# Ordering the scatters of pairs, and normalizing the first two batch elements beside the last expert slots

## The chip, the cores and the metric

One Trainium2 chip; the kernel runs on one of its cores. The metric is the device time of one launch in microseconds (us), as the median over several runs. A core has five engines that each follow their own instruction stream: TensorE (PE in the profile), VectorE (DVE), ScalarE (ACT), GpSimd (POOL) and SyncE (SP). Transfers run on 16 DMA engines and are started by instructions on SP or POOL.

## The reference

Causal attention with 16 heads over four batch elements of 1024 rows of 256 numbers, a layer norm, a mixture of experts (8 experts, each row uses two), and a second layer norm. Cut to what matters here:

```python
# x: (4, 1024, 256)
x = layernorm(x + attention(x))
scores = (x @ router_w.T + router_b) / temp
gates  = sinkhorn(scores)                      # 3 rounds
vals, idx = top_k(gates, 2)
g   = relu(einsum('btd,edf->btef', x, wg))     # wg, wp: (8, 256, 512)
p   = einsum('btd,edf->btef', x, wp)
all = einsum('btef,efd->bted', g * p, wo)      # wo: (8, 512, 256)
x = layernorm(x + sum over the two chosen experts of gate * all)
```

## The kernel before

**Attention.** The four batch elements are worked through in turn. After the attention of an element come its projection, residual and first layer norm (L547 to 557); the normalized rows are stored to two DRAM tables, `x_rows` (what the experts gather) and `results` (what they add to). Then `route` (L688 to 839) works out the gates, the two experts of each row, and the place of each of the 2048 (row, expert) pairs in a DRAM table `pairs`, which holds a region for each expert. `scatter` (L842 to 856) writes these pairs: 16 indirect DMAs per element, issued by POOL. A small hand-written planner (`Lane`, L1061) decides where in the instruction stream each piece is put: a generator yields the cost of what it has just issued (`SCAT`, `SCAT3`, or 1.0 for the last element) and the places in the attention, or in the slots, call `give(budget)`. The Tile scheduler then reorders within the dependencies.

**Slots.** An expert's rows are handled in slots. The lists are
- `first[0..7]`: 512 rows of each expert, from elements 0 to 2 only, so that they can run while the last element is still being routed;
- `second[0..7]`: the next 512 rows of each expert, with rows of all elements, in the fixed order 7, 6, ... 0. The first of them is the same expert as `first[7]` and takes over its split weights (`like`, L1116). All eight pair lists come with one DMA of 64 KB (`ents1`, L977);
- `further`: slots of 256 rows, whose expert and list are read from a table in SBUF into SP registers. Three of them (`SURE`) are always run, any more inside `tc.If(filled > SURE)` (L1238), which this input doesn't enter.

`slot` (L1005) does gate and linear projection (`gp`, `lp`), relu times linear, and the output projection `eo`, each in three fp32r matmuls of high and low halves (L195 to 197). ACT writes the high half, DVE the low half (L188, L189). Each block of 128 output rows is added into `results` by an accumulating indirect DMA that POOL issues (L1039); the adds of a slot wait for those of the slot before (`added`). `begin` (L1204) runs in pieces between the parts of the slot ahead: it reads the pair list of the slot after next on SP, gathers its rows on POOL (L957), transposes and splits the next slot's rows, splits its weights, and loads the weights of the slot after (three DMAs of 512 KB on SP, L983). There is one raw buffer per kind of weight and two of each half, six buffers of `eo`, two of gathered rows.

**Where the last element's scatters go.** In slots `first[5]` and `first[6]`, eight `give(1.0)` each, and what is left behind `first[6]` (`places.until`, L1232). `second[0]`'s list can be read only when the last of them has landed.

**The end.** After the last slot's adds: eight loads of 512 rows (`z`, L1255, SP), statistics on DVE (L1269, L1270), `rstd` and `off` on POOL (L1272 to 1276), normalization on ACT for the first five (L1279) and on DVE for the last three (`DZ` = 3, L1287), and the stores (L1258, SP).

Of the kernel before, what the change touches and what calls it, by code (L numbers as in the profile page):

```python
# [21 lines left out]
XG = 2  # L22
SCAT, SCAT3 = 3.5, 2.5
DZ = 3
HB = 6
# [16 lines left out]
def kernel(  # L42
# [39 lines left out]
    SR = 256  # L82
    REGION = BT + SR
    NOVER = (2 * BT - 4 * ER + 2 * (SR - 1)) // SR
    NLIST = (E - 1) * REGION + 2 * ER + NOVER * SR
# [100 lines left out]
    def split(hi, lo, src, sub=None):  # L186

        nc.scalar.copy(hi, src)  # L188
        (sub or nc.vector).tensor_tensor(lo, src, hi.bitcast(F32), ALU.subtract)  # L189

# [354 lines left out]
    def layernorm(x, n):  # L545
        mv = small.tile([P, BPQ, 2], F32, tag="mv", name=f"mv_{n}", bufs=2)
        for i in range(BPQ):  # L547
            st = small.tile([P, 6], F32, tag="bnst", name=f"bnst_{n}_{i}")
            nc.vector.bn_stats(st, x[:, i, :])
            nc.vector.bn_aggr(mv[:, i, :], st)  # L550
        rstd = small.tile([P, BPQ], F32, tag="rstd", name=f"rstd_{n}", bufs=2)
        spread[0] = nc.gpsimd.tensor_scalar_add(rstd, mv[:, :, 1], EPS_LN)
        nc.gpsimd.tensor_tensor(rstd, rstd, neg_half, ALU.pow)
        for i in range(BPQ):
            nc.vector.tensor_scalar(
                x[:, i, :], x[:, i, :], mv[:, i, 0:1], rstd[:, i : i + 1], ALU.subtract, ALU.mult
            )
# [127 lines left out]
    def route(b):  # L685
# [140 lines left out]
        yield 0.0  # L826
        nc.vector.tensor_tensor(base, base, ps[:, NE : NE + E], ALU.add)
        if b == B - 2:
            nc.vector.tensor_tensor(base, base, floor, ALU.max)
# [12 lines left out]
    def scatter(b, ent, ati):  # L842

        for n in range(NB):
            for k in range(2):
                while not hole[0]:
                    yield WAIT
                ins = nc.gpsimd.indirect_dma_start(  # L848
                    out=pairs[:, :],
                    out_offset=bass.IndirectOffsetOnAxis(ap=ati[:, k, n : n + 1], axis=0),  # L850
                    in_=ent[:, n, k, :], in_offset=None,
                )
                in_turn(ins)
                after(ins, latest[0])
                apart("pairs", "last" if b == B - 1 else "write", ins, ("last", "write", "early"))
                yield SCAT if b < B - 2 else SCAT3 if b < B - 1 else 1.0


    def tab(name, shape):
        return small.tile([1, *shape], F32, tag=name, name=name, bufs=1)  # L860

    shift = tab("shift", [E])
    for e in range(E):
        nc.gpsimd.memset(shift[:, e : e + 1], float(e * REGION + 2 * ER - SR + 1))
    tables = {}

    def lay_out():
# [35 lines left out]
        tables["filled"] = small.tile([1, 1], I32, name="filled", bufs=1)  # L903
        nc.vector.tensor_copy(tables["filled"], upto[:, E - 1 :])
        yield 0.0


    def value(r, s, top):
        return nc.values_load(
            tables["slots"][0:1, r, s : s + 1], engines=[mybir.EngineType.SP], min_val=0, max_val=top,  # L910
            skip_runtime_bounds_check_because="worked out on the chip from counts that add up to 2 * B * T",
        )
# [10 lines left out]
    class Slot:  # L923


        def __init__(self, which, s):
            self.which, self.s, self.name = which, s, f"{which}_{s}"
            self.rows = SR if which == 2 else ER
            self.blocks = self.rows // P
            self.raw, self.hl = [None] * 3, [None] * 3  # L930
            self.like = None

    lists = {}

    def pairs_of(k):
        if k.which == 2:
            row = value(1, k.s, NLIST - SR)
            k.ent = const.tile([P, k.blocks, 4], I32, name=f"ent_{k.name}")
            nc.sync.dma_start(
                out=k.ent, in_=pairs[bass.ds(row, SR)].rearrange("(p j) w -> p j w", j=k.blocks)  # L940
            )
            return
        if k.which not in lists:
            ent = lists[k.which] = const.tile([P, E, k.blocks, 4], I32, name=f"ents{k.which}")
            regions = pairs[: E * REGION].rearrange("(e r) w -> e r w", r=REGION)
            ins = nc.sync.dma_start(
                out=ent.rearrange("p e j w -> p e (j w)"),
                in_=regions[:, k.which * ER : (k.which + 1) * ER].rearrange("e (p j) w -> p e (j w)", p=P),
            )
            if not k.which:  # L950
                apart("pairs", "early", ins, ("last",))
        k.ent = lists[k.which][:, k.s]

    def gather(k):
        k.xg = early.tile([P, ER // P, C], F32, tag="xg", name=f"xg{k.name}", bufs=XG)
        for j in range(k.blocks):
            ins = nc.gpsimd.indirect_dma_start(  # L957
                out=k.xg[:, j], out_offset=None, in_=x1_rows[: BT if k.which else BT - T],
                in_offset=bass.IndirectOffsetOnAxis(ap=k.ent[:, j, 0:1], axis=0),
            )  # L960
            if not k.which:
                in_turn(ins)
# [8 lines left out]
    def weights(k, i):  # L971

        if k.like is not None:
            return
        if k.which == 2:
            if i == 0:
                k.e = value(0, k.s, E - 1)  # L977
            rows_e = bass.ds(k.e, 1)
        else:
            rows_e = slice(k.s, k.s + 1)  # L980
# [4 lines left out]
    def halves(k, i):  # L985
        if k.like is not None:
            k.hl[i] = k.like.hl[i]
            return
        w = k.raw[i]
# [14 lines left out]

    def slot(k, between):  # L1005

        R = k.rows
        hs = []
        for f in range(NFC):
# [13 lines left out]
            )  # L1023
            split(hh, hlo, r)
            hs.append((hh, hlo))
            next(between, None)
            if k in first[E - 3 : E - 1]:
                places.give(1.0)
        mine = []
        h_, l_ = k.hl[2]  # L1030
        for j in range(k.blocks):
# [17 lines left out]
            next(between, None)  # L1049
            if k in first[E - 3 : E - 1]:  # L1050
                places.give(1.0)
# [62 lines left out]
    first = [Slot(0, e) for e in range(E)]  # L1114
    second = [Slot(1, e) for e in reversed(range(E))]
    second[0].like = first[-1]  # L1116
    further = [Slot(2, n) for n in range(NOVER)]
# [79 lines left out]
    for gen in (finish(B - 1, (0,), alone=True), route(B - 1), lay_out()):  # L1197
        drain(gen)
    filled = nc.values_load(
        tables["filled"][0:1, 0:1], min_val=0, max_val=NOVER,  # L1200
        skip_runtime_bounds_check_because="worked out on the chip from counts that add up to 2 * B * T",
# [24 lines left out]

    def run(keys, given=()):
        drain(begin(keys, 0, given))
        for n, key in enumerate(keys):
            slot(key, begin(keys, n + 1, given))  # L1230
            if key is first[E - 2]:
                places.until(f"S{B - 1}")  # L1232

    run(first + second + further[:SURE], (0,))

    experts.close()
    pctx.close()
    with tc.If(filled > SURE):  # L1238
        added.clear()
        with early_pool() as early, ffn_pool() as ffn:  # L1240
            run(further[SURE:])


    zp = ctx.enter_context(tc.tile_pool(name="zp", bufs=1))
    y_rows = out.rearrange("b t c -> (b t) c")
    zs = {}

    def rows_of(of, i, cut=slice(0, BPQ)):

        return of[i * QC : (i + 1) * QC].rearrange("(p n) c -> p n c", p=P)[:, cut]  # L1250

    def load_z(i):
        z = zp.tile([P, CC, FF], F32, tag="z", name=f"z{i}", bufs=BT // QC)
        z = zs[i] = z.rearrange("p k f -> p (k f)").rearrange("p (n c) -> p n c", c=C)
        nc.sync.dma_start(out=z, in_=rows_of(results, i))  # L1255

    def store_z(i, z, cut=slice(0, BPQ)):
        nc.sync.dma_start(out=rows_of(y_rows, i, cut), in_=z[:, cut])  # L1258

    n_z = BT // QC  # L1260
    rest = []
    for i in range(n_z):
        load_z(i)
    for i in range(n_z):
        z = zs.pop(i)
        mv = small.tile([P, BPQ, 2], F32, tag="mv", name=f"mv_f{i}", bufs=2)
        for j in range(BPQ):
            st = small.tile([P, 6], F32, tag="bnst", name=f"bnst_f{i}_{j}")
            nc.vector.bn_stats(st, z[:, j, :])  # L1269
            nc.vector.bn_aggr(mv[:, j, :], st)  # L1270
        rstd = small.tile([P, BPQ], F32, tag="rstdz", name=f"rstd_f{i}", bufs=4)
        nc.gpsimd.tensor_scalar_add(rstd, mv[:, :, 1], EPS_LN / 4)  # L1272
        nc.gpsimd.tensor_tensor(rstd, rstd, neg_half, ALU.pow)
        off = small.tile([P, BPQ], F32, tag="offz", name=f"off_f{i}", bufs=4)
        nc.gpsimd.tensor_tensor(off, mv[:, :, 0], rstd, ALU.mult)
        nc.gpsimd.tensor_scalar(off, off, -1.0, None, ALU.mult)
        if i < n_z - DZ:
            for j in range(BPQ):
                nc.scalar.activation(  # L1279
                    z[:, j, :], z[:, j, :], AF.Identity, bias=off[:, j : j + 1], scale=rstd[:, j : j + 1]  # L1280
                )
            store_z(i, z)
        else:
            rest.append((i, z, rstd, off))
    for i, z, rstd, off in rest:
# [83 lines left out]
```

## Time and profile before

| | us |
|---|---|
| runs: lowest, median, highest of 3 | 1086.51, 1090.79, 1091.84 |
| the profiled execution | 1095.9 |
| its span | 1094.2 |
| attention of the four elements, about | 0 to 760 |
| first TensorE work of the second stage (`xgT` at) | 870.84 |
| adds of three alternate second slots begin | 909.83, 945.59, 981.36 |
| last add issued | 1060.81 |
| first load of z issued | 1068.04 |
| last normalization on DVE ends | 1090.73 |

Windows of the span, in us of busy time of each engine, with TensorE's granted clock as a share of its full one and the mean busy share of the DMA engines:

| stretch | PE | DVE | ACT | POOL | clock | DMA |
|---|---|---|---|---|---|---|
| 818 to 854 (36) | 35.55 | 22.00 | 19.39 | 27.17 | 1.00 | 0.53 |
| 854 to 876 (22) | 3.35 | 2.71 | 2.77 | 13.99 | 0.59 | 0.39 |
| 900 to 1020 (120) | 119.32 | 65.91 | 68.35 | 63.08 | 1.00 | 0.58 |
| 1020 to 1067 (47) | 36.54 | 20.29 | 21.70 | 21.76 | 0.92 | 0.48 |
| 1067 to 1094 (27) | 0.00 | 17.04 | 10.04 | 13.74 | 0.50 | 0.80 |

How to read such lines: a group line gives the kernel line, engine, operation, the tile written and the tile read, how often it ran, busy time and mean, and then how long the engine stood idle just before, and what ended that idle time. "SPq" is a DMA's issue on SP. In the chain of waits each piece is followed back to what released it, so the pieces add up to the span. Idle time of an engine that isn't on that chain costs nothing.

### The profile page before, as it was taken

The numbers are of one execution on the slowest core, as the hardware profiler recorded it, in microseconds if no ns is written. First come the engines' busy times: TensorE is split into PE (matmuls) and PEld (weight loads), VectorE is DVE, ScalarE is ACT, GpSimd is POOL, SyncE is SP. The second block draws the span as 40 slices with busy tenths as digits, with TensorE's granted clock in tenths as the row PEclk, the third lists the DMA queues.
The fourth block names the chain that finished last, engine by engine and source line by source line (L and its number), as shares of the span: only waits on it lengthen the run. The fifth ranks groups of instructions, "written<-read, shape, count | busy, mean of one in ns | idle before, by whom it ended". The sixth has DMA issues, their size and how long they took to land.

```text
span 1094.2 us, 18114 instructions
## 1 busy us (share of the span) xinstructions
PE 975.8 (89%) x6436; PEld 608.2 (56%) x6436; DVE 734.9 (67%) x1622; ACT 625.4 (57%) x1314; POOL 479.1 (44%) x543
## 2 busy tenths in 40 slices
PE   6689999999999999989999996899999399999970
PEld 4555433455544455543444443488888288888860
DVE  4767787888888778787757882286686145555536
ACT  3445666765665755666656663656565145555533
POOL 6177511022352632552223215427557655554535
PEclk9889999999989999999999998999999699999985
DMA  6574420231240330333143220357555345656537
GB/s 245 165 213 121 117 86 18 76 117 33 95 121 17 107 114 5 127 80 98 47 102 98 46 70 2 99 174 186 141 125 123 69 109 113 172 113 164 123 36 307
DMA packets 71363, 119.67 MB, mean 109 GB/s; under 512 B 16416, under 2 KB 43040, under 8 KB 70880
## 3 DMA queue, kind: packets, MB, share of 16 engines
q1 hardware_dynamic: 48544, 81.76, 24.3%
q0 software_dynamic: 20672, 36.41, 15.5%
q8 instruction: 53, 0.87, 0.3%
q10 hardware_dynamic: 2048, 0.27, 0.2%
q14 instruction: 46, 0.38, 0.1%
HBM read 82.52 MB, written 35.60 MB: 108 GB/s over the span
## 4 chain that ended last, share of the span: by engine, by line
PE 74%; DMA 7%; DVE 6%; ACT 5%; SPq 4%; issue 2%; POOL 2%; another core or an unknown queue 1%; ACTq 0%; POOLq 0%; DVEq 0%
PE y L436 12%; PE s L351 11%; PE sT L456 10%; SPq L336 3%; PE gp L197 3%; PE gp L196 3%; PE gp L195 3%; PE eo L197 3%; PE eo L196 3%; PE eo L195 3%; PE po L625 3%; PE lp L197 2%; PE lp L196 2%; ACT pT L467 2%; PE lp L195 2%
## 5 line engine op out<-in xcount | busy, mean ns | idle before, releaser
L467 ACT ACTIVATE pT<-sT 128x512 f32<-128x512 f32 (+1 forms) x608 | 327.1, 575 | 180.8 <-PE sT L456 129.2
L372 DVE TENSOR_REDUCE mx<-s 128x1 f32<-128x384 f32 (+3 forms) x352 | 216.6, 633 | 36.2 <-PE s L368 35.1
L351 PE MATMUL s<-ks,qs 96*128 96x512 bf16 (+3 forms) x768 | 212.4, 333 | 19.4 <-DMA ks<-parts 10.8
L456 PE MATMUL sT<-qs,ks 98*128 98x512 bf16 (+3 forms) x768 | 215.5, 330 | 9.0 <-ACT pT L467 6.9
L381 DVE TENSOR_REDUCE mx<-s 128x1 f32<-128x512 f32 x256 | 171.4, 682 | 47.6 <-PE s L351 47.1
L474 POOL TENSOR_SCALAR_AFFINE_SELECT pT<-pT 128x512 f32<-128x512 f32 x112 | 70.7, 638 | 254.9 <-ACT pT L467 250.4
L436 PE MATMUL y<-pT,va 128*32 128x512 f32 (+3 forms) x1536 | 169.2, 503 | 4.4 <-ACT pT L467 3.1
L1039 POOL DMA_INDIRECT results<-eo,ents x64 | 107.2, 1674 | 82.6 <-ACT eo L1038 65.4
L351 PEld LDWEIGHTS <-qs 96*128 96x128 bf16 x768 | 70.8, 99 | 120.3 <-issue 89.7
L456 PEld LDWEIGHTS <-ks 98*128 98x128 bf16 x768 | 69.8, 99 | 89.6 <-issue 57.4
L848 POOL DMA_INDIRECT pairs<-ent,so_i x64 | 67.8, 1060 | 75.9 <-ACT pT L467 57.5
L368 PE MATMUL s<-mask,ident_b 128*128 128x128 bf16 (+2 forms) x352 | 87.1, 248 | 0.0
L1020 DVE TENSOR_TENSOR relu<-relu,lp 128x512 f32<-128x512 f32 x64 | 43.7, 683 | 60.1 <-ACT relu L1019 30.6
L195 PE MATMUL eo<-wh,hh 128*128 128x256 f32 x280 | 80.5, 289 | 0.9 <-ACT eo L1038 0.6
L957 POOL DMA_INDIRECT xg<-x_rows,ents x64 | 65.1, 1017 | 33.6 <-issue 16.1
L196 PE MATMUL eo<-wl,hh 128*128 128x256 f32 x280 | 79.0, 284 | 0.0
L189 DVE TENSOR_TENSOR wl<-w,wh 128x512 fp32r<-128x512 f32 x108 | 69.3, 684 | 14.3 <-ACT wh L188 13.8
L197 PE MATMUL eo<-wh,hl 128*128 128x256 f32 x280 | 77.7, 284 | 0.0
L1019 ACT ACTIVATE relu<-gp 128x512 f32<-128x512 f32 (+1 forms) x76 | 42.7, 563 | 59.6 <-PE gp L197 49.9
L436 PEld LDWEIGHTS y<-pT,va 128*32 128x32 f32 x1536 | 31.8, 108 | 64.6 <-issue 46.5
L195 PE MATMUL gp<-xh,wh 128*128 128x512 f32 (+1 forms) x176 | 65.0, 376 | 2.1 <-ACT xh L188 1.2
L196 PE MATMUL gp<-xl,wh 128*128 128x512 f32 (+1 forms) x176 | 65.6, 374 | 0.0
(213 smaller groups left out, 1849.0 us busy)
## 6 DMA issues: line engine op xcount, KB each, us to landing
ks<-parts SPq DMA_DIRECT2D x90, 128.0 KB
w<-in_wg_dram SPq DMA_DIRECT2D x18, 512.0 KB
w<-in_wp_dram SPq DMA_DIRECT2D x18, 512.0 KB
w<-in_wo_dram SPq DMA_DIRECT2D x18, 512.0 KB
qs<-parts SPq DMA_DIRECT2D x66, 128.0 KB
parts<-lv POOLq DMA_DIRECT2D x12, 384.0 KB
parts<-lv POOLq DMA_DIRECT2D x24, 192.0 KB
xh<-in_x_t_dram SPq DMA_DIRECT2D x8, 512.0 KB
```

The costliest lines, as they stand in the source:

```text
L195: nc.tensor.matmul(ps, lhsT=sh, rhs=mh, start=(i == 0), stop=False)
L196: nc.tensor.matmul(ps, lhsT=sh, rhs=ml, start=False, stop=False)
L197: nc.tensor.matmul(ps, lhsT=sl, rhs=mh, start=False, stop=(i == n - 1))
L351: nc.tensor.matmul(ps, lhsT=q(h, half)[:NROW, t * P : (t + 1) * P], rhs=k(h, kc)[:NROW, :w], start=first, stop=last,)
L368: nc.tensor.matmul(each[:, :, w - P :], lhsT=ident_b, rhs=mask.unsqueeze(1).to_broadcast([P, m, P]), start=False, stop=True,)
L372: nc.vector.tensor_reduce(mx_of[:, half, h0 : h0 + m, t], each, AX.X, ALU.max)
L381: nc.vector.tensor_reduce(mx_of[:, kc, h, t : t + 1], ps, AX.X, ALU.max)
L436: nc.tensor.matmul(acc[g, qc][SLOT * h : SLOT * (h + 1), lo:], lhsT=va[b % 2][:, kb, at : at + SLOT], rhs=pT[:, h, lo:], start=(kb == 0), ...
L456: nc.tensor.matmul(st[:, h % m * w : (h % m + 1) * w], lhsT=k(h, kb // BPQ)[: NROW + 2, kb % BPQ * P : (kb % BPQ + 1) * P], rhs=q(h, qc)[: ...
L467: latest[0] = nc.scalar.activation(pT[:, h + 1 - m : h + 1, lo:], st[:, : m * w].rearrange("p (h t) -> p h t", t=w), AF.Exp, scale=scale,)
L474: diagonal[0] = nc.gpsimd.affine_select(out=block, in_=block, pattern=[[0, HG], [1, P]], compare_op=ALU.is_ge, fill=0.0, base=0, channel_m ...
L1039: ins = nc.gpsimd.indirect_dma_start(out=results[:, :], out_offset=bass.IndirectOffsetOnAxis(ap=k.ent[:, j, 1:2], axis=0), in_=eo, in_offs ...
```

## The change

1. *Scatters.* Each scatter of pairs is given a dependency on the last but one before it of the same element. `SCAT3` goes from 2.5 to 2.0. The last element's scatters cost 0.5 and not 1.0 per place, and places are given in `first[6]` only.
2. *Order of the second stage.* `order_of_second`, a few operations on one row, runs once, when element 1 has been routed. It picks the expert with the fewest rows of elements 0 and 1 and makes the eight second slots a rotation of the experts that ends with that one. Expert and list are now read into SP registers for each second slot, with one list DMA of 8 KB each; the weights of the first of them are loaded and split anew.
3. *Early end of elements 0 and 1.* In the last second slot, POOL loads the four z tiles of elements 0 and 1, after the adds of the slot before. Their statistics, `rstd` and normalization (all of it on DVE but `rstd`) and their stores on SP are put behind the last split of the further slots 0, 1 and 2. The end then has four tiles and not eight, with `DZ` = 2. If the `If` is entered, those four are loaded and normalized again after it; an expert with over 1024 rows in elements 0 and 1 (`again`) makes the program enter it.
4. In the first layer norm, the instruction that later gathers are scheduled after is the pow and not the add.

```diff
-SCAT, SCAT3 = 3.5, 2.5
-DZ = 3
+SCAT, SCAT3 = 3.5, 2.0
+DZ = 2
...
-        spread[0] = nc.gpsimd.tensor_scalar_add(rstd, mv[:, :, 1], EPS_LN)
-        nc.gpsimd.tensor_tensor(rstd, rstd, neg_half, ALU.pow)
+        nc.gpsimd.tensor_scalar_add(rstd, mv[:, :, 1], EPS_LN)
+        spread[0] = nc.gpsimd.tensor_tensor(rstd, rstd, neg_half, ALU.pow)
...
+        if b == EARLY - 1:
+            order_of_second()
...
+        sent = []
         for n in range(NB):
             for k in range(2):
...
                 after(ins, latest[0])
+                if len(sent) > 1:
+                    after(ins, sent[-2])
+                sent.append(ins)
...
-                yield SCAT if b < B - 2 else SCAT3 if b < B - 1 else 1.0
+                yield SCAT if b < B - 2 else SCAT3 if b < B - 1 else 0.5
...
+    def order_of_second():
+        few = tab("few", [E])
+        nc.vector.tensor_tensor(few, floor[:1], base[:1], ALU.subtract)
+        most, again = tab("most", [1]), tab("again", [1])
+        nc.vector.tensor_reduce(most, few, AX.X, ALU.min)
+        nc.vector.tensor_scalar(again, most, -float(ER), float(NOVER), ALU.is_lt, ALU.mult)
+        tables["again"] = again
+        nc.vector.tensor_reduce(most, few, AX.X, ALU.max)
+        nc.vector.tensor_scalar(few, few, most, None, ALU.is_equal)
...
+        nc.vector.tensor_scalar(seq[:, 1], seq[:, 0], float(REGION), float(ER), ALU.mult, ALU.add)
+        nc.vector.tensor_copy(seqi[:, 1], seq[:, 1])
...
     def pairs_of(k):
-        if k.which == 2:
-            row = value(1, k.s, NLIST - SR)
+        if k.which:
+            row = value(k.table, 1, k.s, NLIST - k.rows)
             k.ent = const.tile([P, k.blocks, 4], I32, name=f"ent_{k.name}")
             nc.sync.dma_start(
-                out=k.ent, in_=pairs[bass.ds(row, SR)].rearrange("(p j) w -> p j w", j=k.blocks)
+                out=k.ent, in_=pairs[bass.ds(row, k.rows)].rearrange("(p j) w -> p j w", j=k.blocks)
             )
             return
...
-            if k in first[E - 3 : E - 1]:
+            if k is first[E - 2]:
                 places.give(1.0)
+        if ahead is not None:
+            ahead()
         mine = []
...
-    second = [Slot(1, e) for e in reversed(range(E))]
-    second[0].like = first[-1]
+    second = [Slot(1, n) for n in range(E)]
...
+    def load_early():
+        for i in range(n_early):
+            z = work.tile([P, T], F32, tag="yT0", name=f"ze{i}", bufs=2) if i < 2 else work.tile(
+                [P, BPQ, C], F32, tag="x1", name=f"ze{i}", bufs=X1_BUFS
+            )
+            z = early_z[i] = z.rearrange("p (n c) -> p n c", c=C) if i < 2 else z
+            with tc.issue_after(further[0].gathered.ins):
+                ins = nc.gpsimd.dma_start(out=z, in_=rows_of(results, i))
+            for o in added:
+                after(ins, o)
+
+    def center_early(i):
+        mv = small.tile([P, BPQ, 2], F32, tag="mve", name=f"mv_e{i}", bufs=n_early)
+        for j in range(BPQ):
+            st = small.tile([P, 6], F32, tag="bnst", name=f"bnst_e{i}_{j}")
+            nc.vector.bn_stats(st, early_z[i][:, j, :])
+            nc.vector.bn_aggr(mv[:, j, :], st)
+        rstd = small.tile([P, BPQ], F32, tag="rstdz", name=f"rstd_e{i}", bufs=4)
+        nc.gpsimd.tensor_scalar_add(rstd, mv[:, :, 1], EPS_LN / 4)
+        nc.gpsimd.tensor_tensor(rstd, rstd, neg_half, ALU.pow)
+        early_z[i] = early_z[i], mv, rstd
+
+    def end_early(i):
+        z, mv, rstd = early_z[i]
+        for j in range(BPQ):
+            nc.vector.tensor_scalar(
+                z[:, j, :], z[:, j, :], mv[:, j, 0:1], rstd[:, j : j + 1], ALU.subtract, ALU.mult
+            )
+        store_z(i, z)
...
+    keys = first + second + further[:SURE]
+    n = keys.index(second[-1])
+    half = n_early // 2
+    run(keys, (0,), {n: load_early}, {
+        n + 1: [(center_early, i) for i in range(half)],
+        n + 2: [(end_early, i) for i in range(half)] + [(center_early, i) for i in range(half, n_early)],
+        n + 3: [(end_early, i) for i in range(half, n_early)],
+    })
```

## The prediction

> **What bounds the kernel now.** I read the page first: engine shares, then the row of granted clock.
>
> ```profile
> PE 975.8 (89%) x6436; PEld 608.2 (56%) x6436; DVE 734.9 (67%) x1622; ACT 625.4 (57%) x1314; POOL 479.1 (44%) x543
> PE   6689999999999999989999996899999399999970
> PEclk9889999999989999999999998999999699999985
> ```
>
> TensorE is busy 89% of the span, so time is found only where its row dips: slice 32 (848 to 875 us) and the last two. Windows of those places have the columns: stretch, its length, busy time of PE, weight loads, DVE, ACT and POOL, clock, DMA share, GB/s.
>
> ```profile
> 860.00:880.00 20.00, 6.94 (x27) 4.93 (x28) 1.29 (x2) 1.55 (x3) 11.99 (x13) 0.54 0.35 78
> 1035.00:1040.00 5.00, 3.37 (x22) 2.96 (x21) 3.36 (x7) 2.23 (x7) 3.39 (x2) 0.87 0.85 167
> 1055.00:1060.00 5.00, 3.70 (x25) 2.93 (x24) 0.85 (x2) 1.61 (x4) 2.03 (x2) 1.00 0.26 31
> 1060.00:1065.00 5.00, 0.00 (x0) 0.00 (x0) 0.00 (x0) 0.13 (x1) 2.05 (x2) 0.76 0.52 65
> ```
>
> There are two holes. The chain of waits over them (start, length, what):
>
> ```profile
> 862.36 2.16 DMA pairs<-ent,so_i
> 864.53 2.60 DMA ents<-pairs
> ...
> 871.82 2.54 DMA xg<-x_rows,ents
> ...
> 1054.44 3.69 DMA results<-eo,ent
> ...
> 1058.95 8.45 DMA results<-eo,ent
> ...
> 1068.90 6.47 DMA z<-results
> ...
> 1089.35 0.41 DVE z L1287
> ```
>
> The *transition* (854 to 876): the second stage cannot gather before the last element's 16 scatters of pairs have landed and the pair list is read back; TensorE stands 16.4 us and then works for some 10 us at half clock. The *tail* (1060 to 1094): the last slot's adds land at 1067.4, then 8 tiles z are loaded, normalized and stored, 26.8 us without a matmul. Everything between runs at one slot per 17.9 us with TensorE full (adds of alternate slots begin at 909.83, 945.59, 981.36).
>
> **The change part by part.** The profiled execution took 1095.9 us (span 1094.2), the median of the runs is 1090.79: a factor of 0.9953. I sum against 1095.9.
>
> *1. At most two scatters in flight, and SCAT3.* A pair scatter issues in 0.97 us with 0.30 between two and lands 2.16 after its start. Two spacings are 2.54 us, more than 2.16, so a wait for the last but one would already be over: 0. The built program's order shows no new wait on the scatters anyway, and the third element's burst of back-to-back scatters (655 to 670) is still there, six and more in a row. Cost 0.
>
> *2. The last element's scatters in one slot.* Before, POOL runs its scatters between adds from 818.6 to 863.3 without rest (scatter 0.97, add 1.58, gaps 0.30), four of them ahead of the sixth slot's first add. In the built order they start after that add (its eo is ready at 824.33) and go two by two between the adds. Filled in with the rows: add 826; four scatters to 831; two adds 835; two scatters 838; one add, two scatters 842; then eo6_0 at 845.06, and three more rounds of add plus two scatters at 4.4 us, to 863–866. POOL loses its early scatters but has the idle gap before 845 to make them up: +0.5. Behind them SP reads one 8 KB list per slot in place of one 64 KB list: between the 2.16 of a scatter and the 2.60 of the 64 KB row: −0.3. But the first three slots of `second` also queue 1 MB of weights just behind these lists, beside the gathers (landing 2.54 when nothing else ran), and ACT has the splits of that weight ahead of those of xg. At 512 KB per 3.3 us (first z of the tail: issued 1068.04, first used 1071.33) they land by 869.5 and 872, and ACT needs xg at 875: hidden, with 2 us of slack; if that goes, each microsecond is on the path, at half clock. I take **+1**, range −1 to +5.
>
> *3. order_of_second.* Thirteen operations on one row of eight numbers, 0.2 us each by routing's 128x8 rows (L756 0.214, L760 0.199), 2.7 us of VectorE once, beside attention where TensorE is 9 tenths busy and VectorE 7 to 8: 0, at most +3.
>
> *4. Second's first slot no longer borrows weights.* 1.5 MB more to load and 6 splits (ACT 0.57, DVE 0.68 each, 7.5 us together), before 875, where ACT works 1.55 and DVE 1.29 of 20 us: 0. The loads run while the seventh slot waits.
>
> *5. Rows and lists per slot.* SP now issues, per slot, list, wg, wp, wo strictly in that order. Before, every other slot's wg and wp were fetched ahead of the wo before it (wg 912.21, wp 914.01, wo 917.02). That wg moves to 918, lands by about 925, and its splits begin at 929.48: hidden, slack 4.5 us. Two register loads per slot lie in the 0.9 us that a further slot already shows between its list (1004.39) and wg (1005.29). 0, range 0 to +14 (rival C).
>
> *6. Early layer norm.* POOL now issues four loads of 512 KB (elements 0 and 1) after the adds of the last but one second slot have landed, and the last slot's adds and the gather of the third further slot stand behind them. POOL's timeline, before:
>
> ```profile
> 1027.90 1.54 POOL L1039 DMA_INDIRECT results<-eo,ents  x1 [3.67 <-DMA results<-eo,ents]
> 1036.61 2.08 POOL L1039 DMA_INDIRECT results<-eo,ents  x1 [0.31 <-ACT relu L1019]
> 1043.56 1.78 POOL L1039 DMA_INDIRECT results<-eo,ent  x1 [4.87 <-ACT hh L188]
> 1058.95 1.55 POOL L1039 DMA_INDIRECT results<-eo,ent  x1 [2.97 <-DMA results<-eo,ent]
> 1060.81 1.55 POOL L1039 DMA_INDIRECT results<-eo,ent  x1 [0.30 <-issue]
> ```
>
> Four issues at 0.84 (row of x_rows' store) put the end of issuing at 1031.3. The tail moved 2 MB in the 7 us after 1068.04; beside weights (DMA 0.62 to 0.99 busy here) I take landing at 1036.5. Here a rule bears: the Trainium skill, "DMA: Bandwidth & Descriptors", Rules for kernel authors, asks an accumulating DMA to wait for an earlier access only of the *same bytes*. The last slot's expert has no rows of elements 0 and 1, so by the rule its adds could start at 1031.3; but the built order shows the first add waiting on the four loads' semaphores. By the rule the delay of that add is 3.4 us, by the program's wait 8.6 us; I count the second. Then, with adds of 1.54 to 2.08: four adds to 1044.7, landed 1046.8; first further slot 1047.3 and 1049.2, landed 1053; second 1053.7 and 1056, landed 1060; third 1060.9 and 1063.5, landed 1070. Two of the idle gaps in the block above (4.87, 2.97) take up most of the 8.6. That is +2.7. On top come POOL's four add+pow pairs (0.23 + 1.05, gaps: 7 us over 20 us where POOL has 12 us of adds) and VectorE's 12 us (per z 1.77 for statistics, 1.38 to normalize; 4 z) in 25 us that hold 12 us of work: part of it falls ahead of relu and splits that TensorE awaits. A second rule speaks against it: "SBUF — State Buffer", Who interferes with whom, says a VectorE tensor_scalar in its two-port mode and a GpSimd operation lock each other out for the whole instruction. 16 normalizations at 0.35 would hold POOL 5.5 us if all met an add; the rows say an add takes 1.54 alone and up to 2.08 beside VectorE, so +0.5 on the two or three that matter. I take **+4** for the last add's landing in all, range +2 to +8.
>
> *7. The tail with four z.* Stores of the early z (2 MB) go beside the third further slot. Four statistics end 1.57 × 4 + about 1 after the first use, at 1078.6 had nothing moved (before: the eighth at 1086.8); POOL's four steps for the last z take 2.0 (0.23 + 1.05 + 0.22 + 0.23 and gaps), the normalization 1.4, and the end comes 3.5 after that as before: 1085.6 in place of 1094.2, **−8.5**, range −10 to −6. ACT has two z left at 2.06 each, the first two, so it is done before.
>
> Sum: +1 + 0 + 4 − 8.5 = −3.5, so 1092.4 profiled, and 1092.4 × 0.9953 = **1087.3**.
>
> **Rivals.** Case A is the sum, 1082 to 1092 from its terms' ranges.
>
> *B: an old stall goes.* The chain has 1% of "another core or an unknown queue": two stalls without a named releaser, the longer one shown here (VectorE in the third element's burst of scatters), the other ACT's 5.23 us at 705.09, during gathers.
>
> ```profile
> 669.62 0.26 DVE L604 RECIPROCAL rec<-yt_ps 128x16 f32<-128x16 f32 x1 [8.70 <-remote]
> ```
>
> Instruction packets move on two queues just there. If these are instruction fetches held up behind POOL's small descriptors, thirteen new VectorE instructions shift the place where the next block is needed. The Trainium skill, "Runtime: NRT & Kernel Launch", Instruction fetch mechanics, calls a block's cost mostly hidden; the row says 8.7. Both gone: −3.5 − 13.9, so 1073.6; the longer alone: about 1078.7. Against it: the burst itself stays, so the shift may as well leave the stall or lengthen it.
>
> *C: slower, by SP's queue in the second stage.* If the weights' slip behind wo exceeds the slack of 4.5 us (list waits, loads beside gathers of 300 GB/s), every slot is paced by its load. At 2 us for each of 7 slots, +14: 1092.4 + 14 = 1106.4, × 0.9953 = 1101. It decides from some 1.3 us per slot on, where it eats the tail's gain and 0.5% more. For it: the order has no slack between lists and weights. Against: one slot in two already runs with wg behind wo (931.4, then 932.64) and TensorE stays full.
>
> *D: the early norm is all there is.* The scatters' new places neither help nor hurt and the adds hide entirely in the gaps (+1 rather than +4): −7.5, 1083.
>
> **How the numbers follow.** What a measurement of this kernel tells from no change is about 0.5%, 5.5 us. Chances: A 0.47, B 0.15, C 0.26, D 0.12. The prediction is A's 1087. Faster by over 0.5% (under 1085.3): B 0.15, most of D 0.09, a quarter of A 0.12, so 0.36; slower: C less a little 0.24 and A's end 0.02, so 0.26; within: 0.38. The range goes down to 1075 (half of B) and up to 1100 (half of C).
>
> **What would show it.** Step 2: last scatter's start within 862 to 866, TensorE's hole 15 to 20 us. Step 5: alternate adds still 35.75 us apart. Step 6: POOL's first add of the last second slot 8 to 9 us behind the landing of the slot before, last add landed 2 to 8 us later relative to that. Step 7: 18 us from there to the end in place of 26.8. A shifted stall in the third or fourth element's attention, or a longer slot period, would make the prediction wrong.

## The result and the profile after

The changed kernel takes 1104.49 us (median of 6 runs, 1102.91 to 1105.82) and the kernel before 1089.85 (1086.51 to 1091.84): a ratio of 1.014 with a 95% interval of 1.0121 to 1.0158. It is **slower by 1.4%**. In a later set of runs, beside a median of before of 1077.86, the same pair gave 1.0103 (1.0055 to 1.0151). The profiled execution took 1105.16 us, span 1103.5, 9.3 more than that of before. The medians are 14.6 us apart; the profiled execution of before lay 6 us above its median, so the traces divide 9.3 us and not all of the 14.6.

The page after, first the lines that answer to those of before:

```profile
PE 980.0 (89%) x6436; PEld 613.6 (56%) x6436; DVE 744.0 (67%) x1654; ACT 622.7 (56%) x1308; POOL 478.5 (43%) x539
PE   6689999999999999999999986999999299999870
PEclk9899999999999999999999997899999599999985
```

TensorE's work has hardly changed (980.0 us for 975.8, same count). The dip in slice 32 has gone from 3 to 2, and the end, `970` in the last three slices before, is `870`: neither has closed. Windows (stretch, length, PE, weight loads, DVE, ACT, POOL, clock, DMA share, GB/s) of the same places:

```profile
860.00:880.00 20.00, 3.41 (x10) 2.10 (x11) 3.52 (x6) 3.36 (x6) 12.49 (x12) 0.50 0.58 174
1040.00:1060.00 20.00, 16.20 (x119) 15.62 (x119) 9.58 (x34) 7.41 (x19) 10.18 (x9) 0.91 0.53 132
1060.00:1080.00 20.00, 7.68 (x41) 6.98 (x39) 11.64 (x38) 3.12 (x8) 11.49 (x10) 0.78 0.55 122
```

TensorE finished at 1059 before; now it still has 7.68 us of work after 1060, with holes in it. Lined up on marks that both traces have, the 9.3 us divide like this. A second pair of traces, both from one later set of runs (e5 and e6 below: both kernels unchanged, spans 1078.7 and 1089.6), gives the same division:

| stretch | first pair | second pair |
|---|---|---|
| up to the last eo of `first[6]` on ACT | +0.6 | +0.5 |
| from there to the first eo of `first[7]` (the transition) | +3.4 (24.9 to 28.3) | +3.05 (25.35 to 28.4) |
| from there to the last add of the last but one second slot | −0.45 | +0.6 |
| from there to the last add of all | **+10.7** (38.7 to 49.4) | **+11.0** (36.9 to 47.8) |
| last add's start to the first load of z | +2.35 (7.2 to 9.6) | +2.7 |
| first load of z to the end | −7.3 (26.2 to 18.9) | −6.9 |

So the end did become shorter as meant, and the last four slots with the step from the last add to the first load of z gave nearly twice that back. POOL's timeline there, after:

```profile
1025.68 3.29 POOL L1069 DMA_INDIRECT results<-eo,ent  x1 [1.25 <-ACT eo L1068]
1034.60 2.25 POOL L1301 DMA_DIRECT2D ze<-results  x4 [5.64 <-DMA results<-eo,ent]
1037.15 1.09 POOL L989 DMA_INDIRECT xg<-x_rows,ent  x1 [0.30 <-PE gp L199]
...
1047.21 1.63 POOL L1069 DMA_INDIRECT results<-eo,ent  x1 [7.22 <-ACT xh L190]
...
1055.02 1.05 POOL L1314 TENSOR_TENSOR rstd_e<-rstd_e,neg_half 128x4 f32<-128x4 f32 x1
...
1060.85 1.77 POOL L1069 DMA_INDIRECT results<-eo,ent  x1 [0.20 <-issue]
1066.59 1.56 POOL L1069 DMA_INDIRECT results<-eo,ent  x1 [3.97 <-ACT hh L190]
```

The four early loads are out by 1036.85, but the add behind them starts only at 1047.21: it waits for 2 MB to land. (xh is named because ScalarE's update was the last one before the start. In the trace this add waits on the four semaphores of the early loads; in e4 below, where these waits are taken out, it follows the loads at once.) Meanwhile rstd of the early tiles (POOL) stands behind those adds, and VectorE stands at the normalization that needs rstd, with relu and splits of the last slot after it in its stream. VectorE's timeline and what TensorE waited for (engine, line, waited for: us, times, longest):

```profile
1056.10 1.38 DVE L1320 TENSOR_SCALAR ze<-ze,mv_e,rstd_e 128x256 f32<-128x256 f32 x4 [2.56 <-POOL rstd_e L1314]
1060.69 1.51 DVE L1320 TENSOR_SCALAR ze<-ze,mv_e,rstd_e 128x256 f32<-128x256 f32 x4 [3.20 <-POOL rstd_e L1314]
```

```profile
PE gp L197 <- DVE relu L1048: 5.1, 2, 4.7
PE xgT_ps L1030 <- DMA xg<-x_rows,ent: 3.3, 1, 3.3
```

TensorE waits twice that it did not before (its longest wait in these slots was 1.2 us): 3.3 us for the gather of the third further slot, which was issued behind the early loads, and 4.7 us for VectorE. After each its granted clock falls to 0.50 for some microseconds, here after the second:

```profile
1066.00:1067.00 1.00, 1.00 (x6) 1.00 (x6) 1.00 (x4) 0.51 (x2) 0.41 (x1) 0.50 0.06 16
```

### The profile page after: what moved, and what is told of

The parts are those of the page before. It is cut to its first block, busy times and chain, and to the rows that moved or that the text cites. A ratio compares the mean times of both kernels' runs of the same rounds, so it can differ in the third digit from the quotient of the medians.

```text
span 1103.5 us, 18205 instructions
## 1 busy us (share of the span) xinstructions
PE 980.0 (89%) x6436; PEld 613.6 (56%) x6436; DVE 744.0 (67%) x1654; ACT 622.7 (56%) x1308; POOL 478.5 (43%) x539
## 5 line engine op out<-in xcount | busy, mean ns | idle before, releaser
L374 DVE TENSOR_REDUCE mx<-s 128x1 f32<-128x384 f32 (+3 forms) x352 | 216.7, 633 | 36.1 <-PE s L370 35.0
L458 PE MATMUL sT<-qs,ks 98*128 98x512 bf16 (+3 forms) x768 | 216.5, 332 | 15.0 <-ACT pT L469 13.4
L383 DVE TENSOR_REDUCE mx<-s 128x1 f32<-128x512 f32 x256 | 171.3, 681 | 43.5 <-PE s L353 42.3
L191 DVE TENSOR_TENSOR wl<-w,wh 128x512 fp32r<-128x512 f32 x114 | 73.6, 684 | 37.5 <-ACT wh L190 35.0
L854 POOL DMA_INDIRECT pairs<-ent,so_i x64 | 64.7, 1011 | 72.8 <-ACT pT L469 49.2
L1069 POOL DMA_INDIRECT results<-eo,ent x38 | 64.5, 1698 | 46.6 <-ACT eo L1068 19.8
L190 ACT CAST wh<-w 128x512 fp32r<-128x512 f32 x114 | 64.0, 618 | 23.1 <-DMA w<-in_wg_dram 16.5
L1069 POOL DMA_INDIRECT results<-eo,ents x32 | 53.6, 1674 | 42.2 <-ACT eo L1068 30.2
```

The lines of the kernel that those rows point to most:

```text
L191: return (sub or nc.vector).tensor_tensor(lo, src, hi.bitcast(F32), ALU.subtract)
L374: nc.vector.tensor_reduce(mx_of[:, half, h0 : h0 + m, t], each, AX.X, ALU.max)
L383: nc.vector.tensor_reduce(mx_of[:, kc, h, t : t + 1], ps, AX.X, ALU.max)
L458: nc.tensor.matmul(st[:, h % m * w : (h % m + 1) * w], lhsT=k(h, kb // BPQ)[: NROW + 2, kb % BPQ * P : (kb % BPQ + 1) * P], rhs=q(h, qc)[: ...
L1069: ins = nc.gpsimd.indirect_dma_start(out=results[:, :], out_offset=bass.IndirectOffsetOnAxis(ap=k.ent[:, j, 1:2], axis=0), in_=eo, in_offs ...
```

## The experiments

The kernels came in four sets (e1 to e4, e5 to e8, e9 to e11, e12 and e13), each on one chip beside the kernel before, so ratios are compared and not microseconds: the median of before was 1079.37, 1077.86, 1088.75 and 1081.21. The stretches in microseconds are each from a single trace; two traces of the kernel before differ by 1.8 us in the last stretch of adds (38.7 and 36.9) and by 1.1 us from the last add to the first load of z (7.2 and 6.2).

### Which part costs it

**e1**, without the early norm (all eight z at the end, three on VectorE):

```diff
-    n_early = EARLY * T // QC
+    n_early = 0
-DZ = 2
+DZ = 3
```

> The changed kernel without its early layer norm: no z tile is loaded in the last second slot, the end has eight tiles with three on VectorE as before; scatters and order of the second stage as changed. Theory 1 (the early norm's own waits in the last slots cost more than the shorter tail brings): 1093 to 1098 us, and the adds of the last second slot follow the slot before without the 12 us hole. Theory 2 (the scatters' new places and the half clock after them cost it): stays at 1101 or above. Theory 3 (the new order's lists and weights on SP pace the second stage): also 1101 or above.

**e2**, the scatters as before, early norm and order kept:

```diff
-SCAT, SCAT3 = 3.5, 2.0
+SCAT, SCAT3 = 3.5, 2.5
-                if len(sent) > 1:
-                    after(ins, sent[-2])
-                sent.append(ins)
-                yield SCAT if b < B - 2 else SCAT3 if b < B - 1 else 0.5
+                yield SCAT if b < B - 2 else SCAT3 if b < B - 1 else 1.0
-            if k is first[E - 2]:
+            if k in first[E - 3 : E - 1]:
                 places.give(1.0)
...
+            if key is first[E - 2]:
+                places.until(f"S{B - 1}")
```

> The changed kernel with the scatters as before (2.5 and 1.0 per place, in two slots, no limit of two, the rest placed behind the seventh slot); early norm and order kept. Theory 1: 1101 to 1103, only the 3 us of the transition come back. Theory 2: 1092 to 1096. Theory 3: unchanged, 1104.

**e3**, both edits: what is left is the order of the second stage, with the 13 operations of `order_of_second` and part 4 of the change.

> Neither the early norm nor the new places of the scatters: what is left of the change is the order of the second stage with its lists and loads per slot. Theory 1: within 3 us of before, 1088 to 1093. Theory 2: the same. Theory 3: 1097 or above.

| | ratio to before | 95% interval |
|---|---|---|
| e3: order | 1.0032 | 1.0011 to 1.0054 |
| e1: order and scatters | 1.0050 | 1.0030 to 1.0071 |
| e2: order and early norm | 1.0082 | 1.0053 to 1.0112 |
| e6: all three (next set) | 1.0103 | 1.0055 to 1.0151 |

The microseconds that I had expected were for the first comparison, where before takes 10 us more; read as ratios, theory 1 expected 1.003 to 1.007 for e1 and got 1.005. Theories 2 and 3 would have kept e1 at the whole loss. e2, expected at 1.010 to 1.012 by theory 1, 1.002 to 1.006 by theory 2 and 1.013 by theory 3, lies between the first two, and e3 at the upper edge of theory 1's 0.998 to 1.003, under the 1.007 of theory 3: the early norm is the largest part, 0.5% (e2 less e3), but the order costs 0.3% that theory 1 did not have, and the scatters 0.2% (e1 less e3, whose intervals overlap; the transition below shows them in the traces). They add up to the whole within its interval. No run takes the order apart from the 13 operations and from part 4; e12 and e13 below keep part 4 without the order and are level with the kernel before.

> The changed kernel, unchanged, beside the others on one chip. If its parts add up (order 0.3%, scatters 0.2%, early norm 0.5%, from the first three experiments), the ratio is 1.010; if the 1.4% of the first comparison came in part from stalls of that chip, 1.008 to 1.011; if the parts make each other worse, 1.014 again.

e6 is the changed kernel unchanged: 1.0103, what the sum of the parts gives. Its interval (four runs) also holds the 1.008 to 1.011 of the reading by stalls and the 1.014 of the third, so it does not tell them apart.

### The waits of the early norm

**e4**: the adds of the last second slot are told that the early loads touch other rows.

```diff
             for o in added:
                 after(ins, o)
+            apart(f"results{second[-1].name}", "early_z", ins, ())
...
-            apart(f"results{k.name}", "add", ins, ("add",))
+            apart(f"results{k.name}", "add", ins, ("add", "early_z"))
```

> The changed kernel, but the adds of the last second slot don't wait for the four early loads (they touch other rows). Theory 1, if this wait is the main part: the first of these adds starts at about 1038 and not 1047, the last add 5 to 9 us earlier, 1096 to 1100. If VectorE's wait for rstd and the crowded transfers set it instead: 1102 to 1105.

Measured 1.0067 (1.0047 to 1.0087), within the 1.006 to 1.009 that the first reading's microseconds come to as a ratio; the last add came 3.7 us earlier than in e6, not the 5 to 9 expected. POOL's timeline:

```profile
1025.24 2.24 POOL L1301 DMA_DIRECT2D ze<-results  x4 [5.44 <-DMA results<-eo,ent]
1027.79 1.94 POOL L1069 DMA_INDIRECT results<-eo,ent  x1 [0.30 <-ACT wh L190]
1030.04 1.46 POOL L989 DMA_INDIRECT xg<-x_rows,ent  x1 [0.30 <-issue]
```

The add follows the loads at once instead of 10 us later, and TensorE's wait for VectorE falls from 5.1 to 0.4 us, so that wait was a consequence of the held adds. From the last but one second slot's last add to the last add of all it is 44.2 us; e6 has 47.8, e1, without the early norm, 38.5. So of the 9.3 us between e6 and e1 the hold is 3.7, and 5.6 remain. The largest piece of them that the trace shows is a transfer: the gather of the third further slot, issued behind the 2 MB, still keeps TensorE waiting 3.4 us, and its granted clock is 0.50 from 1038 to 1040, after that wait:

```profile
1036.65 0.30 PE L1030 MATMUL xgT_ps<-ident,xg 128*128 128x128 f32 x1 [3.37 <-DMA xg<-x_rows,ent]
```

**e9**: normalization and stores of the last two early tiles behind the loads of z, that is behind the `If`.

```diff
-        n + 3: [(end_early, i) for i in range(half, n_early)],
...
         nc.sync.dma_start(out=zs[i], in_=rows_of(results, i))
+    for i in range(half, n_early):
+        end_early(i)
```

> The changed kernel with one thing moved: the normalization and stores of the last two early z stand behind the four loads of z at the end, so that the If before these loads (a join: the first load waits for all engines and all transfers issued before it) has no early stores to wait for. If the join is part of the cost: from the last add's start to the first load of z some 6 us and not 8.8 to 9.6, and the ratio 0.2 to 0.4% under the changed kernel's 1.010. If not: 1.010.

From the last add's start to the first load of z: 5.74 us. With the early stores ahead of the `If` it was 9.58, 8.84, 8.80 and 7.85 (changed kernel twice, e2, e4), without any early norm 5.4 to 5.5 in e1, e3 and e7, and 7.2 and 6.2 in the two traces of before. So stores ahead of the `If` cost **2 to 4 us** there. The ratio, 1.0126 (1.0092 to 1.016), is 0.14% under the first comparison's 1.014, in a set with nearly the same median of before; the intervals overlap, and the expected 1.006 to 1.008 was missed: the traces show this cost and the ratio alone does not.

How it arises, SP's own waits show (columns as for TensorE above). In the changed kernel, before, and e9 (L1344 and L1238 are the line of the `If`):

```profile
SPq L1344 <- SPq L1344: 7.8, 2, 6.0
```

```profile
SPq L1255 <- DMA results<-eo,ent: 26.8, 1, 26.8
SPq L1238 <- SPq L1238: 4.3, 1, 4.3
```

```profile
SPq L1367 <- DMA results<-eo,ent: 12.4, 1, 12.4
SPq L1344 <- SPq L1344: 3.9, 1, 3.9
```

The branch of the `If` stands in SP's stream behind the stores. Before and in e9 SP passes it early, at 1035.6 and 1060.3, and the last thing that it waits for is the landing of the adds. In the changed kernel SP reaches it at 1075.6, once the last early store, which needs VectorE's normalization, is issued (1074.35). Its next instruction runs 6.0 us after the branch starts (3.8 to 6.0 in all fifteen traces), and a further 1.8 us pass behind it. So here it was the branch's late place, and not the landing of the stores, that held the first load. What SP does in these 4 to 6 us the trace does not say.

**e10**, e4 and e9 together:

> The changed kernel with both waits taken out: the last second slot's adds don't wait for the early loads, and the last two early stores stand behind the loads of z. If the two waits are what the early norm costs: near the kernel without early norm less some of the shorter end, 1.002 to 1.005. If crowding of the transfers and of VectorE is: 1.006 to 1.009.

1.0083 (1.0051 to 1.0114), last add to first z 5.73, last stretch of adds 44.5 as in e4. Within this set e9 and e10 differ by the hold alone: 4.4 us in the traces, 0.43% in the ratio. The two waits together are worth 0.6% against the 1.014 of the first comparison, which has the stalls of the last section as this set has, and 0.2% against e6, which has not. The rest stayed, as the reading by crowded transfers and VectorE expected; those two were not taken apart.

### The transition

**e7**: order only (e3), with the first second slot's gathers ahead of the next slot's weights.

```diff
+        if k is second[1] and i == 0:
+            for o in second[0].gathers:
+                after(ins, o)
```

(`ins` is that slot's first load of weights, with the two others behind it on SP; `gathers` is the list of the gathers.)

> Order of the second stage alone (no early norm, scatters as before), and the three loads of weights that follow the first list (512 KB each) wait until the gathers of the first second slot have landed. If these loads slow the gathers (gather to first transpose 2.84 us before, 6.1 us after), that time falls to about 3 us and the ratio to 0.999 to 1.001; if the order costs through the second stage's lists on SP, it stays at 1.003.

SP's timeline and TensorE's first transpose, first in the changed kernel, then in e7:

```profile
867.01 1.20 SPq L972 DMA_DIRECT2D ent<-pairs  x2
868.76 0.38 SPq L1014 DMA_DIRECT2D w<-in_wg_dram  x1
869.39 0.38 SPq L1014 DMA_DIRECT2D w<-in_wp_dram  x1
870.00 0.37 SPq L1014 DMA_DIRECT2D w<-in_wo_dram  x1
```

```profile
875.52 0.69 PE L1030 MATMUL xgT_ps<-ident,xg 128*128 128x128 f32 x2 [20.52 <-DMA xg<-x_rows,ent]
```

```profile
849.91 1.20 SPq L969 DMA_DIRECT2D ent<-pairs  x2
859.21 0.38 SPq L1012 DMA_DIRECT2D w<-in_wg_dram  x1
```

```profile
855.36 0.69 PE L1031 MATMUL xgT_ps<-ident,xg 128*128 128x128 f32 x2 [14.96 <-DMA xg<-x_rows,ent]
```

From the first gather's issue to that transpose: 6.1 us in the changed kernel (869.43), 6.9 in e3, 2.9 in e7, 2.8 before. The three weights, 1.5 MB behind the list, do slow the gathers by 3 to 4 us. But the ratio is 1.0035 (1.0012 to 1.0057), as e3's, where 0.999 to 1.001 had been expected; of the 4 us only 1.0 reaches the first eo of `first[7]` (25.4 us after the last eo of `first[6]`, e3 26.4, before 24.9 and 25.35). So this is not what the order costs in the median, and what is stays open: the traces of e3 and of before (e5) differ by 1.1 us here and 1.6 in the last slots, and a single profiled execution places the attention anywhere within some 8 us (the last eo of `first[6]` at 839.0 to 846.9 in the ten traces without the stalls told of below).

The scatters: from the last eo of `first[6]` to the first gather it is 13.9 to 14.4 us in the six traces with the new places (e1, e4, e6, e9, e10 and the changed kernel) and 12.0 to 12.1 in e2, e3 and e7 (old scatters, new lists). With the old scatters and one long list it is 13.4 and 13.6 in the two traces of before and 12.4 to 12.5 in e8, e11, e12 and e13 below. The new places cost about 2 us, and one list per slot gives 0.3 to 1.5 back.

### A better place

**e8** is the changed kernel with the scatters, the order and the borrowed weights put back as before (these lines are left out below). The four early z are loaded behind the last gather and the last second slot's adds, nobody waits for them, and everything else of the early norm stands behind the last split. The stores are issued by ScalarE (ACTq in the view below).

```diff
-            with tc.issue_after(further[0].gathered.ins):
+            with tc.issue_after(further[SURE - 1].gathered.ins):
                 ins = nc.gpsimd.dma_start(out=z, in_=rows_of(results, i))
...
-        store_z(i, z)
+        nc.scalar.dma_start(out=rows_of(y_rows, i), in_=z)
...
-    run(keys, (0,), {n: load_early}, {
...
+    run(keys, (0,), {n + 1: load_early}, {
+        n + 3: [(center_early, i) for i in range(n_early)] + [(end_early, i) for i in range(n_early)],
+    })
```

> Built on the kernel before (scatters, static order and borrowed weights as before) with an early norm placed otherwise: the four z of elements 0 and 1 are loaded behind the last gather and the last second slot's adds, the further slots' adds don't wait for them, and all of their statistics, rstd and normalization stand behind the last slot's last split, the stores on ScalarE's queue. Theory 1 (only the place of the early norm cost time, the shorter end is real): last add within 2 us of before, end 6 to 7 us shorter, ratio 0.993 to 0.997. If any norm beside the last slots costs what the end gains: 0.999 to 1.003.

1.0082 (1.005 to 1.0115): theory 1 as I had put it missed, and the trace shows where.

```profile
1050.50 1.78 POOL L1061 DMA_INDIRECT results<-eo,ent  x1 [0.20 <-issue]
```

```profile
1052.19 9.02 ACTq L1318 DMA_DIRECT2D out_dram<-ze  x4
```

```profile
1064.88 1.77 SPq L1356 DMA_DIRECT2D z<-results  x4
```

The last stretch of adds is 45.6 us, 7 to 9 over before where 2 had been expected: two steps of rstd on POOL stand ahead of the last add, and the rest of it was not taken apart. And the first load of z came 14.4 us after that add and not 5.4 to 7.2. SP had passed the branch at 1017.9; its waits behind it end at 1057.79, 1060.37 and 1063.65, and the second and the fourth early store landed at 1057.78 and 1063.64. So here, other than in the changed kernel, the first load did wait for the landing of the early stores. What stands ahead of the `If` is what e9 then tested on the changed kernel.

**e11** loads on SP's queue, keeps only statistics and rstd before the `If`, and normalizes (two on VectorE, two on ScalarE) and stores behind the loads of z. **e12** moves rstd behind them too (the two lines leave `center_early`):

```diff
     def end_early(i):
         z, mv, rstd, off = early_z[i]
+        nc.gpsimd.tensor_scalar_add(rstd, mv[:, :, 1], EPS_LN / 4)
+        nc.gpsimd.tensor_tensor(rstd, rstd, neg_half, ALU.pow)
```

**e13** is e12 with two early tiles and six at the end (`n_early = 2`).

> Built on the kernel before (its scatters, static order, borrowed weights): the four early z are loaded on SP's queue behind the last second slot's adds, nobody waits for them; statistics and rstd behind the last split, before the If; normalization (two on VectorE, two on ScalarE) and stores behind the loads of the last four z. Theory 1: last add within 2 us of before, first load of z too, end 5 to 7 us shorter: ratio 0.993 to 0.997. If 2 MB of loads beside the last slots' adds cost what the end gains: 0.999 to 1.003.

> As the split norm before it (on the kernel before, four early z loaded on SP's queue in the first further slot, statistics before the If), but rstd is worked out behind the loads of the last four z too, so that neither POOL's last add nor the join waits for POOL's pows. If the pows cost what the trace of the split norm shows (some 1.5 us before the last add and 4 us at the join): ratio 0.998 to 1.001. If only the loads beside the adds count: 1.004 as there.

> The same with two early z (the first element) and six at the end: 1 MB of early loads and not 2. If the loads lengthen the landing of the further slots' adds by their bytes (the four took 7 us), half of it goes: last add about 1 us behind the kernel before, end some 4 us shorter, ratio 0.996 to 0.999. If the delay doesn't follow the bytes: at or above the kernel with four.

| | ratio | 95% interval | last stretch of adds | last add to z | z to end |
|---|---|---|---|---|---|
| before (first trace) | | | 38.7 | 7.2 | 26.2 |
| before (second trace) | | | 36.9 | 6.2 | 25.8 |
| e11 | 1.0039 | 1.0014 to 1.0064 | 43.5 | 9.2 | 20.75 |
| e12 | 1.0012 | 0.9997 to 1.0028 | 41.4 | 5.5 | 20.75 |
| e13 | 0.9993 | 0.9974 to 1.0012 | 38.8 | 5.4 | 23.0 |

e11 missed both of its readings, upward, and its trace showed the pows (rstd's `pow` on POOL) between the last two adds and ahead of the join, the step from the last add to the first load of z; e12 and e13 came out just above the upper edge of their first readings (1.0012 for 1.001, 0.9993 for 0.999). By these single traces the pows cost 2.1 us ahead of the last add and 3.8 at the join; halving the early bytes cut the last stretch by 2.6 us, and the end grew by 2.2. The best form of the early norm is no faster than the kernel before, within 0.3%. No version that was run beats it clearly.

> The kernel before, unchanged, for a trace of it on the chip of these runs. If the two stalls of the attention (8.70 us on VectorE, 5.23 us on ScalarE, releaser unknown) belong to one chip, they are missing here and the profiled execution is 10 us or more shorter, about 1080; if they belong to the program, they are there, at the same instructions, and it is near 1095.

e5, the kernel before once more, has none of the two stalls; see the last section.

## Why the prediction was wrong

It forecast 1087 (the sum: −3.5) and the time is 1104.5, outside the range. In profiled time it is +9.3 for −3.5: of the 12.8 us between, step 2 has 2.4, step 6 has 6.7, the step from the last add to the first load of z, which had no term, 2.35, and step 7 has 1.2. Point by point, on the first pair of traces:

- **Step 1**, the limit of two: 0, as said; the trace shows no new wait for it.
- **Step 2**, the transition: +1 forecast, +3.4 measured, inside its range of −1 to +5. Last scatter at 864.29, in the 862 to 866 that was named; TensorE's hole is 20.5 us, just over the 15 to 20. Of the +3.4, 0.8 lie ahead of the first gather (new places about +2, lists less) where +0.2 was forecast, and 2.6 behind it, where the weights were called "hidden, with 2 us of slack". That was a question of when ScalarE's splits end; what the weights do to the gathers was left out (1.5 MB are issued there, not 1): from the first gather to the first transpose it is 6.1 us for 2.8 before. e7 gives back 1.0 of the 2.6; the rest stays open.
- **Steps 3 to 5**: +0.6 up to the transition, −0.45 over the second stage. Rival C (the queue on SP paces each slot) did not happen: alternate adds of the second stage still come 35.95 to 36.1 us apart (912.60, 948.59, 984.69, 1020.64). That its 1101 is the number nearest to the result is luck.
- **Step 6** failed, and it decides: +4 forecast, +10.7 and, from the last add to the first load of z, +2.35 measured. Three things were wrong in it. First, the wait for the early loads: their landing was put 5.2 us after the last issue and the first add 8.6 us behind the landing of the slot before; measured are 10.4 and 12.6, with 324 to 362 GB/s moved from 1036 to 1044, beside weights and gathers. (They also began 6.7 us later than the 1027.9 that was copied from the trace of before. But 3.5 of that was carried over from the transition, and 3.2 is the add ahead of them, which takes 3.3 us for 2.1 to issue and lands later. It does so in every trace but those of before, without an early norm too, so it is no part of this step; why was not tried.) Second, VectorE was priced by its work (12 us in 25). That part of this falls ahead of relu and splits was said, but what hurt was an instruction that waits for POOL with the last slot's relu behind it. Third, the `If` was not priced at all: the stores were said to go "beside the third further slot", with no thought of what stands behind them on SP.
- The weighing of the rule in step 6 (the Trainium skill, "DMA: Bandwidth & Descriptors", Rules for kernel authors: an accumulating DMA must wait for an earlier access of the same bytes) took the right side, the program's wait. e4 is the other side: without the wait, which the rule does not ask for, the add starts 0.3 us after the loads, 2.6 us behind the landing of the slot before, for 3.4 in the estimate by the rule.
- The second rule weighed there, the lock between VectorE and GpSimd, was given +0.5; no run isolates it.
- **Step 7**: −8.5 forecast, −7.3 measured, inside −10 to −6. Counted from the last add's start (the forecast counted from its landing), the end is only 5.0 us shorter.
- **The range of case A**: 1082 to 1092 is not what its terms' ranges give. Their upper ends (+5, +8, −6) come to 1098.
- **Rival B**, a stall that goes: in the changed kernel's trace the stalls are there (13.56 us on ScalarE the longest, up to 6.48 on VectorE), and the time up to the transition is the same, +0.6. That instruction packets move "just there" was misread: in the trace of before none falls into either stall.

The forecast had the mechanism of step 6 in view, a POOL queue held by loads, and stopped at the adds. The chain went on: held adds, rstd behind them, VectorE behind rstd, TensorE behind VectorE, and a half clock behind that.

## What to carry to other kernels

Work moved beside a busy stretch is priced by what its own waits hold up on each in-order engine that it is put on, one engine after the other, and by what it puts ahead of a later branch in the same stream, here the `If` behind the stores on SP. A transfer of some megabytes put beside short dependent ones (gathers, accumulating adds) is priced by their landing beside it, not by its own size; here the time from gather to first use rose from 2.8 to 6.1 us beside 1.5 MB of weights. Where an end of the kernel is shortened by n us, the same n is the budget for all of this, and here it was spent almost twice.

## What was not expected of the hardware

The two stalls without a named releaser in the attention (8.70 and 5.23 us before) are not the program's alone. One to three such stalls, of 4.6 to 13.7 us, are in the five traces taken in the first comparison and in the set of e9 to e11, where before takes 1088.75 to 1089.85 us, and none in the ten of the other three sets, where it takes 1077.86 to 1081.21. The kernel before has 1094.2 us of span with them and 1078.7 without (e5), and its program is the same. VectorE's line in e9, where the first scatters of the third element's burst run:

```profile
661.96 0.26 DVE L606 RECIPROCAL rec<-yt_ps 128x16 f32<-128x16 f32 x1 [8.01 <-remote]
```

In the first comparison both kernels have them, in the set of e5 and e6 neither, so the ratio hardly knows of them; the median of one kernel moves by 1% between sets. e5 to e8, without stalls, and e9 to e11, with them, are recorded under the same chip number, so as far as that number goes they do not belong to one chip, the reading that e5 came out for. What the stalls wait for stays open. The forecast's guess was fetched instructions; in the five stalls of VectorE no packet of the two instruction queues moves, which speaks against it and does not settle it.
